# An attention and mixture-of-experts kernel: 48 expert tiles of five blocks first, results of three blocks read back early, ten half blocks at the end

## The chip, the cores and the metric

The kernel runs on one core of a Trainium2 chip, in one program. The metric is the device time of one execution in microseconds; lower is better. In the profile PE is TensorE (matmuls and transposes), PEld its weight loads, DVE is VectorE, ACT is ScalarE, POOL is GpSimd and SP is SyncE, which issues most DMAs. All arithmetic is in float32.

## The reference

The input x has 4 sequences of 1024 tokens with 256 features; the context has 4 sequences of 77 rows. Cut to what matters:

```python
h = layernorm(x)
x = x + cross_attention(h, ctx)        # 16 heads of 64, softmax over 77 keys, + h, a second layernorm
f = layernorm(x)                       # 4096 tokens
weights, indices = top_k(softmax(f @ Wg), 4)     # 32 experts
for e in range(32):
    pos = pairs (token, expert) with expert e, in order of token, at most 2048 of them
    xg = f[token of pos]
    y[token of pos] += (silu(xg @ W1[e]) * (xg @ W3[e]) @ W2[e]) * weight
z = silu(f @ Ws1) * (f @ Ws3) @ Ws2    # a shared expert, for every token
out = x + y + z
```

So there are 4096 × 4 = 16384 pairs of token and expert, and which pair goes to which expert is known only when the gate has been computed.

## The kernel before

**Blocks.** The 4096 tokens are 8 blocks of 512 (`NB`, `TB`), each of 4 chunks of 128. The first part of the program (lines 773 to 883, 32 steps `t`, one for each chunk) does the attention, and two blocks behind it the gate, the choice of four experts (`choose`, `mark`), the counting (`count`) and the placing (`place`) of every pair. `cums[b]` holds, for each expert, how many pairs the blocks before b have given it.

**Rows.** `send` (L685) scatters each token's normalised row to DRAM (`xr`), four times, once for each of its experts: 16 indirect DMAs for a block, issued by GpSimd. In `xr` each expert has its own stretch, filled in order of token.

**Expert tiles.** A tile is 128 rows of one expert. The expert part (lines 1222 to 1294) is a pipeline of four steps over tiles j: `expert_in` (two transposes on PE, gT copied by VectorE, L1131 and L1133), `expert_mid` (four matmuls L1139, silu on ScalarE, product h on VectorE), `expert_turn` (a transpose), `expert_out` (two matmuls L1163, the result scaled to y, and scattered by GpSimd to `ys` in DRAM, L1172, one row for each pair). In step j of the loop tile j is in `expert_in`, j − 1 in `expert_mid`, and so on. Rows come in groups of 8 tiles: `fetch` (L1077, on SP's queue, 8 DMAs, asked for 7 steps ahead), and `find` computes in three steps where each row's result goes (`place_`, L1118 or L1124).

**Two tables.** Which expert a tile belongs to and where its rows begin is computed on the chip, because it depends on the counts. Table "a" covers the first `NA` tiles. They are full tiles of rows of the first `BA` blocks, so that they may be fetched when the scatters of these blocks (`early`) have landed. Table "z" covers all later tiles, whose fetches wait for every scatter. An expert's last tile in it may be partly filled: it is read shifted back, and rows that came before are sent to places behind the results (`behind`, `again`, L1122 to L1124). Before the change `NA` is 64 and `BA` 6.

**Early results.** The tables put tiles with rows of the first `BE` blocks first: when `NE_` = `NA` + 32 tiles are done, all results of these blocks are in `ys`. Then they are read back: `take(i)` (L1194, on SP's queue, 512 KB: a chunk's 128 tokens with four results each) and `add_taken` (on VectorE: step 0 adds two pairs of results, L1204; steps 1 and 2 add the two sums to the residual `y0`, L1206). Three chunks are in flight; take i + 3 is issued behind the last add of chunk i. Before the change `BE` is 4, `NE_` 96, the takes begin in step 99, the adds in step 102, in turns of two and one a step. Up to tile `NE_` VectorE scales the results (L1168), from there on ScalarE (L1171).

**Number of tiles.** 128 tiles always run. How many more are needed depends on the counts; a Switch (L1276) goes to the code for that number. In this run it is 16 more, 144 in all.

**The end.** Behind the Switch (lines 1323 to 1360) the results of the blocks not taken early are read by half blocks: `gather` (L1307, 1 MB, on SP's queue, waits for all results) and `gathered` (three operations on VectorE, L1315 to L1317). Between them the shared expert of blocks 3, 4 and 5 is computed: `shared_in` (L715, PE), `shared_mid` (L730, VectorE), `shared_out` (L741, PE), `shared_add` (L754, VectorE). `store` writes half a block out, mostly on ScalarE's queue. Half block hb is half of block hb // 2.

**Order.** `as_written` makes every engine keep the order in which the program is written, except that neighbouring row scatters, and neighbouring result scatters, are free among themselves; operations of the end that need nothing from behind the Switch may be put ahead of it. In the program before, the last nine adds stand so on VectorE, beside tile 127.

Of the kernel before, what the change touches and what calls it, by code (L numbers as in the profile page):

```python
# [9 lines left out]
F32 = mybir.dt.float32  # L10
# [3 lines left out]
ALU = mybir.AluOpType  # L14
AX = mybir.AxisListType

P = 128
# [3 lines left out]
TOPK = 4  # L21
# [9 lines left out]
def kernel(  # L31
# [23 lines left out]
    nc = tc.nc  # L55
    T, D = x.shape
# [6 lines left out]
    NB = T // TB  # L63
# [4 lines left out]
    NJ = T * TOPK // P + NE  # L68


    NA, BA = 64, 6
    NM_ = T * TOPK // P


    BE = 4
    NE_ = NA + NE
    assert BE * TB * TOPK // P + NE <= NE_
    NV = 2 * NE
# [46 lines left out]
    for i in range(2):  # L125
# [13 lines left out]
    nc.gpsimd.memset(none, 0.0)  # L139
    nc.gpsimd.memset(none[:, IDX : IDX + TOPK], -1.0)  # L140
    nc.gpsimd.memset(none[:, OFF : OFF + 1], 1.0)
    behind = const.tile([P, NJ], F32, name="behind")
    nc.gpsimd.iota(
        behind,
        [[P, NJ]],
        base=T * TOPK,
        channel_multiplier=1,
        allow_small_or_imprecise_dtypes=True,
    )
# [623 lines left out]
    with as_written():  # L773
        for t in range(NT):
            blk, c = t // NC, t % NC
            ffn, old = blk - 1, blk - 2
            ahead = blk + 1 < NB
            if c == 0 and blk + 2 < NB:
                xts[blk + 2] = load(blk + 2)
            if t == 0:  # L780

                nc.sync.dma_start(xr[NE * PLACES :, :], none)
                nc.sync.dma_start(
                    xr[: NE * PLACES, :].rearrange("(e q) r -> q e r", q=PLACES)[:P],
                    none.unsqueeze(1).to_broadcast([P, NE, ROW]),
                )
            if t == 18:
                nc.sync.dma_start(ws13[:, :, 0, :], Ws1.rearrange("(k p) f -> p k f", p=P))
                nc.sync.dma_start(ws13[:, :, 1, :], Ws3.rearrange("(k p) f -> p k f", p=P))
                nc.sync.dma_start(ws2, Ws2.rearrange("(k p) f -> p k f", p=P))  # L790
            if t in parts:
                load_experts(*parts[t])
            if c == 1 and ahead:
                scale_in(blk + 1)
            if c == 1 and ffn >= 0:
                measure_out(ffn, 2, 4)
            if c == 3 and ahead:
                bias_in(blk + 1)
            if c == 3:
                measure_out(blk, 0, 2)  # L800
            if c == 3 and ffn >= 0:
                measure_ffn(ffn)
            if c == 1 and old >= 0:
                gate(old)
            if c == 3 and old >= 0:
                count(old)
            sv = [scores(t, g) for g in range(2)]
            if c == 1 and old >= 0:
                turn_gate(old)
                chances(old)  # L810
            soften(t, 0, sv[0])
            if c == 1 and old >= 0:
                powers(old)
            soften(t, 1, sv[1])
            sv.append(scores(t, 2))
            if t >= 1:
                for i in range(3):
                    turn_p(t - 1, i)
            soften(t, 2, sv[2])
            if c == 0 and old >= 0:  # L820
                turn_ffn(old)
            if c == 2 and ahead:
                turn_in(blk + 1)
            if c == 0 and ahead:
                measure_in(blk + 1)
            if c == 1 and old >= 0:
                choose(old)
            if c == 2 and old >= 0:
                mark(old)
            if c == 2 and old + 1 == BE:  # L830
                pairs_of("e", BE)
            if c == 3 and old >= 0:
                place(old)
            invert(t)
            divide(t)
            if c == 1 and ahead:
                norm_in(blk + 1)
            if c == 3 and ffn >= 0:
                norm_ffn(ffn)
            if c == 3:  # L840
                settle(blk, 0)
            elif ffn >= 0:
                settle(ffn, c + 1)
            if c >= 2 and ahead:
                keep(blk + 1, 2 * c - 4, 2 * c - 2)
            if t >= 11:
                b11, c11 = divmod(t - 11, NC)
                send(b11, c11 * TOPK, (c11 + 1) * TOPK)
            if t >= 1:
                residual(t - 1, output(t - 1))  # L850

        sxs[0] = late.tile([P, NC, D], F32, tag="qb", name="sx_0", bufs=3)
        sxs[0] = sxs[0].rearrange("p c d -> p (c d)").rearrange("p (k t) -> p k t", k=KC)
        nc.sync.dma_start(sxs[0], xnd[0])
        z, y = NB - 1, NB - 2
        assert BA == y
        pairs_of("a", BA)
        left = [(y - 1, i) for i in range(NK)]  # L860

        def sends(n):
            for blk, i in left[:n]:
                send(blk, i, i + 1)
            del left[:n]

        del left[:4]
        measure_out(z, 2, 3)
        settle(z, 1)
        sends(3)  # L870
        turn_ffn(y)
        for i in range(3):
            turn_p(NT - 1, i)
        settle(z, 2)
        residual(NT - 1, output(NT - 1))
        measure_out(z, 3, 4)
        gate(y)
        turn_gate(y)
        chances(y)
        powers(y)  # L880
        settle(z, 3)
        sends(2)
        measure_ffn(z)
# [202 lines left out]
    def find(j, step):  # L1086
# [17 lines left out]
        elif step == 1:  # L1104
            cw = bp.tile([P, RG, 2, TOPK], F32, tag="cw", name=f"cw_{j}")
            nc.vector.tensor_tensor(
                cw,
                g[:, :, CODE : CODE + 2 * TOPK].rearrange("p g (i k) -> p g i k", k=TOPK),
                n[1].unsqueeze(2).to_broadcast([P, RG, 2, TOPK]),
                ALU.mult,  # L1110
            )
            own = bp.tile([P, RG, 2], F32, tag="own", name=f"own_{j}")
            nc.vector.tensor_reduce(own, cw, AX.X, ALU.add)
            n.append(own)
        else:
            place_ = bp.tile([P, RG], I32, tag="place", name=f"place_{j}")
            if n[2] is None:
                nc.vector.tensor_copy(place_, n[3][:, :, 0])  # L1118
            else:

                far = bp.tile([P, RG], F32, tag="far", name=f"far_{j}")
                nc.vector.tensor_tensor(far, behind[:, j : j + RG], n[3][:, :, 0], ALU.subtract)  # L1122
                nc.vector.tensor_tensor(far, far, n[2], ALU.mult)
                nc.vector.tensor_tensor(place_, n[3][:, :, 0], far, ALU.add)  # L1124
            n.append(place_)
# [96 lines left out]
    with as_written():  # L1222
        fetch(0)
        fetch_shared(1, nc.sync)
        for j in range(NM_ + len(steps)):
# [23 lines left out]
                shared_out(1)  # L1249
            if j == 7:  # L1250
                shared_add(1)
            if NE_ + 6 <= j < NM_:
                for i, step in adds[: 1 + (j + 1) % 2]:
                    add_taken(i, step)

                    if step == TOPK // 2 and i % HC == 0 and HC <= i <= 2 * NC:
                        store(i // HC - 1, nc.sync)
                del adds[: 1 + (j + 1) % 2]
            if j < NM_ and j % RG in (0, 1, 2):
                find(j // RG * RG, j % RG)  # L1260
            if j == NM_ - 2 * RG:
# [10 lines left out]
                tc.switch_hint(more, (NJ - NM_) // RG + 1, label="more")  # L1272
            if j == NM_ + 2:
                fetch_shared(5, nc.scalar)
    ahead = groups[NM_ // RG][0]
    for n in tc.Switch(more, (NJ - NM_) // RG + 1, hint="more"):  # L1276
        end = NM_ + n * RG
# [20 lines left out]


    hs = ctx.enter_context(tc.tile_pool(name="hs2", bufs=2))  # L1300
    tl = ctx.enter_context(tc.tile_pool(name="tl", bufs=8))
    ysk = ys[: T * TOPK, :].rearrange("(b c p k) d -> b p c k d", c=HC, p=P, k=TOPK)

    def gather(hb):
# [13 lines left out]

    NS = NB - 2
    order = [*range(2 * NS, 2 * NB), *range(2 * BE, 2 * NS)]
    with as_written():
        come = [gather(hb) for hb in order]
        shared_in(3, 0, AF.Silu)
        shared_in(3, 1, AF.Silu)
        for i, step in adds:
            add_taken(i, step)
        shared_mid(3, 0)
        store(4)  # L1330
        shared_mid(3, 1)
        shared_in(4, 0, AF.Silu)
        store(5)
        shared_out(3)
        gathered(*come[0])
        shared_mid(4, 0)
        shared_in(4, 1, AF.Silu)
        shared_add(3)
        gathered(*come[1])
        shared_mid(4, 1)  # L1340
        for hb in (6, 7, 12, 13):
            store(hb)
        shared_in(5, 0, AF.Silu)
        shared_out(4)
        gathered(*come[2])
        shared_mid(5, 0)
        shared_in(5, 1, AF.Silu)
        gathered(*come[3])
        shared_add(4)
        shared_mid(5, 1)  # L1350
        for hb in (14, 15):
            store(hb)
        shared_out(5)
        gathered(*come[4])
        store(8)
        gathered(*come[5])
        store(9)
        gathered(*come[6])
        gathered(*come[7])
        shared_add(5, store)  # L1360


# [53 lines left out]
```

## Time and profile before

| what | value |
| --- | --- |
| time, median of 3 runs | 762.22 us (761.46 to 765.76) |
| the profiled execution's own time | 762.67 us |
| its span, first to last instruction | 760.9 us |
| mean granted TensorE clock | 0.990 |
| PE busy | 719.1 us, 95% |
| VectorE busy | 510.6 us, 67% |
| ScalarE busy | 356.7 us, 47% |
| GpSimd busy | 406.6 us, 53% |
| DMA | 111.98 MB, mean 147 GB/s |
| tiles 0 to 127 and the Switch | about 443 to 690 us of the span |
| the end behind the last tile | 717 to 760.9 us |

A row of a timeline reads: start in us from the span's start, length in us, engine, line, operation, what is written and read, how many; in brackets how long the engine was idle before it and what ended the idle time. A row of the DMA queue's waits reads: who waited, for whom, us in total, how often, the longest. Matmul ends are modelled, so PE counts as busy when it merely follows one matmul on another.

### The profile page before, as it was taken

The numbers are of one execution on the slowest core, as the hardware profiler recorded it, in microseconds if no ns is written. First come the engines' busy times: TensorE is split into PE (matmuls) and PEld (weight loads), VectorE is DVE, ScalarE is ACT, GpSimd is POOL, SyncE is SP. The second block draws the span as 40 slices with busy tenths as digits, with TensorE's granted clock in tenths as the row PEclk, the third lists the DMA queues.
The fourth block names the chain that finished last, engine by engine and source line by source line (L and its number), as shares of the span: only waits on it lengthen the run. The fifth ranks groups of instructions, "written<-read, shape, count | busy, mean of one in ns | idle before, by whom it ended". The sixth has DMA issues, their size and how long they took to land.

```text
span 760.9 us, 12980 instructions
## 1 busy us (share of the span) xinstructions
PE 719.1 (95%) x3512; PEld 535.7 (70%) x3512; DVE 510.6 (67%) x1447; ACT 356.7 (47%) x1634; POOL 406.6 (53%) x491
## 2 busy tenths in 40 slices
PE   6999999999999999999998999999999999988993
PEld 4775767677777777777674567888888887756762
DVE  1874476677787778786767646666677767754376
ACT  0647756676757766667652111222222234534410
POOL 2002344335877777777788775555565565533400
PEclk9999999999999999999999999999999999999997
DMA  8940000130416241331418644466655569962295
GB/s 281 331 127 1 0 1 2 29 110 31 149 44 224 82 135 55 96 109 59 156 53 254 208 150 137 135 193 207 201 164 167 170 221 312 312 227 74 75 398 206
DMA packets 78996, 111.98 MB, mean 147 GB/s; under 512 B 10124, under 2 KB 63808, under 8 KB 78912
## 3 DMA queue, kind: packets, MB, share of 16 engines
q1 hardware_dynamic: 61023, 68.24, 29.1%
q0 software_dynamic: 13056, 36.72, 13.2%
q10 hardware_dynamic: 4832, 6.07, 2.3%
q8 instruction: 32, 0.52, 0.3%
q14 instruction: 53, 0.43, 0.2%
HBM read 62.36 MB, written 48.64 MB: 146 GB/s over the span
## 4 chain that ended last, share of the span: by engine, by line
PE 72%; DVE 10%; ACT 6%; DMA 4%; POOL 3%; issue 3%; SPq 0%; DVEq 0%; POOLq 0%; ACTq 0%
PE po L508 15%; PE peh L1139 14%; PE sc L441 13%; PE py L1163 7%; PE ph L715 6%; ACT p L457 5%; PE pgT L1131 3%; PE pz L741 3%; PE phT L1153 2%; PE pp L490 2%; DVE mx L449 1%; DMA gx<-ys 1%; POOL xr L685 1%; PE pvo L273 1%; PE pvo L298 1%
## 5 line engine op out<-in xcount | busy, mean ns | idle before, releaser
L1172 POOL DMA_INDIRECT ys<-y,place x144 | 141.3, 982 | 118.0 <-ACT y L1171 46.4
L457 ACT ACTIVATE p<-sc,mx 128x77 f32<-128x77 f32 x512 | 159.5, 353 | 93.0 <-DVE mx L449 93.0
L1139 PE MATMUL peh<-we,gT 128*128 x576 | 150.4, 384 | 7.0 <-DVE gT L1133 7.0
L508 PE MATMUL po<-we,pT 128*128 128x256 f32 (+1 forms) x640 | 147.3, 383 | 4.6 <-DVE pT L495 4.3
L685 POOL DMA_INDIRECT xr<-xn,row x128 | 128.1, 1001 | 35.6 <-issue 32.7
L472 POOL TENSOR_TENSOR p<-p,su 128x385 f32<-128x385 f32 (+1 forms) x96 | 91.2, 976 | 97.2 <-DVE su L467 76.5
L441 PE MATMUL sc<-we,qT 128*128 128x385 f32 (+1 forms) x384 | 138.9, 509 | 0.9 <-POOL qT L427 0.9
L508 PEld LDWEIGHTS po<-we,pT 128*128 128x128 f32 (+1 forms) x640 | 118.4, 190 | 26.9 <-DVE pT L495 7.9
L1147 ACT ACTIVATE h<-peh 128x128 f32<-128x128 f32 x144 | 39.9, 278 | 173.1 <-PE peh L1139 165.4
L457 ACT ACTIVATION_READ_ACCUMULATOR p<-sc,mx 128x1 f32 x512 | 119.6, 234 | 0.0
L1139 PEld LDWEIGHTS peh<-we,gT 128*128 128x128 f32 x576 | 98.8, 191 | 17.5 <-DVE gT L1133 9.2
L441 PEld LDWEIGHTS sc<-we,qT 128*128 128x128 f32 x384 | 71.1, 189 | 54.3 <-issue 27.7
L1148 DVE TENSOR_TENSOR h<-peh,h 128x128 f32<-128x128 f32 x144 | 41.8, 290 | 70.8 <-ACT h L1147 70.3
L1163 PE MATMUL py<-we,ehT 128*128 x288 | 86.5, 383 | 0.0
L449 DVE TENSOR_REDUCE mx<-sc 128x5 f32<-128x385 f32 (+1 forms) x96 | 54.4, 576 | 33.3 <-PE sc L441 32.4
L1133 DVE COPY gT<-pgT 128x256 f32<-128x256 f32 x144 | 59.8, 416 | 12.6 <-PE pgT L1131 12.6
L1131 PE MATMUL pgT<-ident,g 128*128 128x128 f32 x288 | 55.2, 274 | 0.8 <-PE py L1163 0.5
L1163 PEld LDWEIGHTS py<-we,ehT 128*128 128x128 f32 x288 | 43.8, 192 | 11.9 <-issue 1.0
L1131 PEld LDWEIGHTS pgT<-ident,g 128*128 128x128 f32 x288 | 40.2, 141 | 16.6 <-issue 2.2
L1168 DVE TENSOR_SCALAR y<-py,own 128x256 f32<-128x256 f32 x96 | 46.4, 483 | 0.1
L490 PEld LDWEIGHTS pp<-ident,p 128*128 128x128 f32 x320 | 36.1, 139 | 11.4 <-issue 5.5
L715 PE MATMUL ph<-sx,ws 128*128 128x512 f32 x96 | 42.9, 595 | 0.0
(221 smaller groups left out, 945.2 us busy)
## 6 DMA issues: line engine op xcount, KB each, us to landing
g<-xr SPq DMA_DIRECT2D x144, 136.0 KB
gx<-ys SPq DMA_DIRECT2D x16, 512.0 KB
gy<-ys SPq DMA_DIRECT2D x8, 1024.0 KB
xr<-y SPq DMA_DIRECT2D x1, 4352.0 KB
y<-in_x SPq DMA_DIRECT2D x8, 512.0 KB
xnd<-xnT SPq DMA_DIRECT2D x6, 512.0 KB
we<-in_W SPq DMA_DIRECT2D x8, 384.0 KB
out<-y ACTq DMA_DIRECT2D x12, 256.0 KB
```

The source lines that it names most:

```text
L441: nc.tensor.matmul(sc[:, : (h1 - h0) * SK], qTs[blk][:, k, o : o + P], mq[:, b, k, h0 * SK : h1 * SK], start=(k == 0), stop=(k == KC - 1),)
L449: nc.vector.tensor_reduce(mx[:, h0:h1], sv, AX.X, ALU.max, negate=True)
L457: nc.scalar.activation(probs[t][:, h, :], sv[:, h - h0, :], AF.Exp, bias=mx[:, h : h + 1], accum_out=su[:, h : h + 1],)
L472: nc.gpsimd.tensor_tensor(p[:, h0:h1, :], p[:, h0:h1, :], su[:, h0:h1].unsqueeze(2).to_broadcast([P, h1 - h0, SK]), ALU.mult,)
L508: nc.tensor.matmul(po[:, :D], pT[:n, i, :], vo[b][:n, i, :], start=(i == 0), stop=(i == KT - 1))
L685: sct = nc.gpsimd.indirect_dma_start(out=xr, out_offset=bass.IndirectOffsetOnAxis(ap=row[:, i : i + 1], axis=0), in_=xn[:, c, :], in_offse ...
L715: nc.tensor.matmul(ph[i], ws13[:, k, i, f * P : (f + 1) * P], xnT[:, k, :], start=(k == 0), stop=(k == KC - 1),)
L1131: nc.tensor.transpose(pt[:, k * P : (k + 1) * P], g[:, j % RG, k * P : (k + 1) * P], ident)
L1133: nc.vector.tensor_copy(gT.rearrange("p k t -> p (k t)"), pt[:, :D])
L1139: nc.tensor.matmul(ph[:, : 2 * H], gT[:, k, :], we[:, ds(ev[j] * EW + k * 2 * H, 2 * H)], start=(k == 0), stop=(k == KC - 1),)
L1163: nc.tensor.matmul(py[:, :D], hT, we[:, ds(ev[j] * EW + KC * 2 * H, D)], start=True, stop=True)
L1172: sent = nc.gpsimd.indirect_dma_start(out=ys, out_offset=bass.IndirectOffsetOnAxis(ap=place_[:, i : i + 1], axis=0), in_=y, in_offset=None,)
```

## The change

`NA` goes from 64 to 48, `BA` from 6 to 5 and `BE` from 4 to 3, so `NE_` from 96 to 80. The counts for table "a" are copied when the placing of block 4 is marked (in step t = 26), no longer after the attention loop. `behind` is held only for the tiles of table "z", and is read by the position in that table. The takes begin in step 83, the adds in step 88, one a step; 36 adds, the last in step 123. None are left for the end. The half blocks 6 and 7 (block 3) are now gathered at the end, ten in all, in the order 12, 13, 6, 7, 14, 15, 8, 9, 10, 11, with ten buffers. Stores follow their half blocks.

```diff
-    NA, BA = 64, 6
+    NA, BA = 48, 5
     NM_ = T * TOPK // P
-    BE = 4
+    BE = 3
...
-    behind = const.tile([P, NJ], F32, name="behind")
+    behind = const.tile([P, NJ - NA], F32, name="behind")
     nc.gpsimd.iota(
         behind,
-        [[P, NJ]],
-        base=T * TOPK,
+        [[P, NJ - NA]],
+        base=T * TOPK + NA * P,
...
-            if c == 2 and old + 1 == BE:
-                pairs_of("e", BE)
+            if c == 2 and old + 1 in (BE, BA):
+                pairs_of("e" if old + 1 == BE else "a", old + 1)
...
-        assert BA == y
-        pairs_of("a", BA)
...
-                nc.vector.tensor_tensor(far, behind[:, j : j + RG], n[3][:, :, 0], ALU.subtract)
+                nc.vector.tensor_tensor(far, behind[:, jt : jt + RG], n[3][:, :, 0], ALU.subtract)
...
-            if NE_ + 6 <= j < NM_:
-                for i, step in adds[: 1 + (j + 1) % 2]:
+            if NE_ + 8 <= j < NM_:
+                for i, step in adds[:1]:
                     add_taken(i, step)
...
-                del adds[: 1 + (j + 1) % 2]
+                del adds[:1]
...
-    tl = ctx.enter_context(tc.tile_pool(name="tl", bufs=8))
+    tl = ctx.enter_context(tc.tile_pool(name="tl", bufs=10))
...
-    order = [*range(2 * NS, 2 * NB), *range(2 * BE, 2 * NS)]
     with as_written():
-        come = [gather(hb) for hb in order]
+        come = {hb: gather(hb) for hb in (12, 13, 6, 7, 14, 15, 8, 9, 10, 11)}
         shared_in(3, 0, AF.Silu)
         shared_in(3, 1, AF.Silu)
-        for i, step in adds:
-            add_taken(i, step)
         shared_mid(3, 0)
         store(4)
         shared_mid(3, 1)
         shared_in(4, 0, AF.Silu)
         store(5)
         shared_out(3)
-        gathered(*come[0])
+        gathered(*come[12])
         shared_mid(4, 0)
         shared_in(4, 1, AF.Silu)
         shared_add(3)
-        gathered(*come[1])
+        gathered(*come[13])
         shared_mid(4, 1)
-        for hb in (6, 7, 12, 13):
-            store(hb)
+        store(12)
+        store(13)
         shared_in(5, 0, AF.Silu)
         shared_out(4)
-        gathered(*come[2])
+        gathered(*come[6])
         shared_mid(5, 0)
         shared_in(5, 1, AF.Silu)
-        gathered(*come[3])
+        gathered(*come[7])
         shared_add(4)
         shared_mid(5, 1)
-        for hb in (14, 15):
+        store(6)
+        store(7)
+        shared_out(5)
+        for hb in (14, 15, 8, 9):
+            gathered(*come[hb])
             store(hb)
-        shared_out(5)
-        gathered(*come[4])
-        store(8)
-        gathered(*come[5])
-        store(9)
-        gathered(*come[6])
-        gathered(*come[7])
+        gathered(*come[10])
+        gathered(*come[11])
         shared_add(5, store)
```

More of the change, by code (lines that the diff above doesn't have):

```diff
@@ L1274 @@
                 fetch_shared(5, nc.scalar)
+    assert not adds
     ahead = groups[NM_ // RG][0]
@@ L1317, in gathered @@
         nc.vector.tensor_tensor(y, y, g[:, :, 1, :], ALU.add)
-    NS = NB - 2
-    order = [*range(2 * NS, 2 * NB), *range(2 * BE, 2 * NS)]
     with as_written():
-        come = [gather(hb) for hb in order]
+        come = {hb: gather(hb) for hb in (12, 13, 6, 7, 14, 15, 8, 9, 10, 11)}
         shared_in(3, 0, AF.Silu)
         shared_in(3, 1, AF.Silu)
-        for i, step in adds:
-            add_taken(i, step)
         shared_mid(3, 0)
```

## The prediction

> **What bounds the kernel now.** I read the page's slices first (PE is 90% busy or more in almost every one), then the busy time of each engine stage by stage, then PE's order of time where it is not full, then VectorE's order of time at the end.
>
> The stages, in the order of columns stretch, length, PE, PEld, DVE, ACT, POOL, clock, DMA share, GB/s:
>
> ```profile
> core 0: us, PE busy (x) PEld busy (x) DVE busy (x) ACT busy (x) POOL busy (x), PEclk, DMA share, GB/s
> ...
> 385.00:444.00 59.00, 52.68 (x235) 33.36 (x233) 38.78 (x134) 18.54 (x61) 47.51 (x60) 1.00 0.58 190
> ...
> 480.00:612.00 132.00, 132.00 (x732) 111.53 (x731) 92.17 (x296) 35.13 (x162) 77.71 (x81) 1.00 0.57 179
> 612.00:673.00 61.00, 56.19 (x300) 45.77 (x299) 44.52 (x140) 28.22 (x97) 35.56 (x34) 1.00 0.90 295
> 673.00:690.00 17.00, 13.22 (x44) 7.43 (x43) 7.47 (x22) 3.78 (x11) 3.12 (x3) 0.95 0.54 156
> ...
> 717.00:749.00 32.00, 31.52 (x98) 18.07 (x96) 20.03 (x26) 4.16 (x8) 1.92 (x2) 1.00 0.88 337
> 749.00:761.00 12.00, 0.00 (x0) 0.00 (x0) 7.93 (x11) 0.00 (x0) 0.00 (x0) 0.67 0.26 91
> ```
>
> From 480 to 612 PE is never idle: the expert tiles run at PE's pace. From 612 to 673, where results of the first four blocks are read back and added, PE loses 4.8 us and the DMA share is 0.90. In the last 12 us PE is done and VectorE works alone. So two places can move: the stretch of the taken results, and the end.
>
> PE's order of time gives the price of the first place:
>
> ```profile
> 616.22 1.03 PE L1139 MATMUL peh<-we,gT 128*128 x4
> ...
> 626.66 1.13 PE L1139 MATMUL peh<-we,gT 128*128 x4 [0.51 <-DVE gT L1133]
> ...
> 649.31 1.13 PE L1139 MATMUL peh<-we,gT 128*128 x4 [0.75 <-DVE gT L1133]
> ...
> 668.09 1.03 PE L1139 MATMUL peh<-we,gT 128*128 x4
> 671.59 1.13 PE L1139 MATMUL peh<-we,gT 128*128 x4 [1.93 <-DVE gT L1133]
> ```
>
> These are tiles 97, 103, 115, 126 and 127. Undisturbed a tile takes 1.6275 us (tile 13 at 479.51 to tile 97 at 616.22: 84 steps). From 616.22 to 668.09 there are 29 steps, 47.20 us at that pace; they took 51.87. The last step took 3.50, where 1.41 would do (no further tile is turned in, 0.22 less). Together 4.67 + 2.09 = 6.76 us lost. Tiles 112 and 113 (642.76 and 645.03; 0.67 and 0.64 too late) come behind the loading of `more` and the hint for the Switch, at the end of step 112; these 1.31 us stay. The other 5.4 us hang on the takes: VectorE waits for the first one (0.67), has two adds in every other step (0.69 and 0.42 us beside 0.42 for gT and 0.29 for h, some ten steps at 0.03 to 0.44), waits in L1124 (0.92, 0.53) and, at the last step, for takes 13 to 15 (2.09; their nine adds stand ahead of h of tile 127 on VectorE).
>
> The end, on VectorE:
>
> ```profile
> 744.91 0.69 DVE L730 TENSOR_TENSOR hT<-ph,sg 128x512 f32<-128x512 f32 x1 [2.42 <-PE ph L715]
> 745.51 1.22 DVE L1315 TENSOR_TENSOR gy<-gy 128x1024 f32<-128x1024 f32 x1
> 746.76 0.69 DVE L1316 TENSOR_TENSOR y<-y,gy 128x512 f32<-128x512 f32 x1
> 747.49 0.69 DVE L1317 TENSOR_TENSOR y<-y,gy 128x512 f32<-128x512 f32 x1
> 748.10 1.22 DVE L1315 TENSOR_TENSOR gy<-gy 128x1024 f32<-128x1024 f32 x1
> ...
> 755.86 1.28 DVE L754 TENSOR_TENSOR y<-pz,y 128x512 f32<-128x512 f32 x2
> ```
>
> PE hands over the last half of block 5 at 744.9. Behind it stand four half blocks, 2.59 us each (745.51 to 748.10), then the shared expert's sum, and 3.8 us for the last store. This is a bare chain: whatever is added behind 744.91 is paid in full.
>
> **The change, part by part.** The profiled execution took 762.67 us for a span of 760.9; the median of the runs is 762.22, 0.45 less. I sum against the profiled execution and carry the difference over.
>
> *Fewer blocks ahead of the first tile: 0.* The first fetch no longer needs the twelve row scatters of block 5, but they were not what it waited for:
>
> ```profile
> SPq L1055 <- DVE r_tab_a L981: 17.7, 1, 17.7
> ```
>
> SP waited for the table of offsets and issued at 426.44; the tiles then wait for PE, which comes to them in its own order at 443.54. The PE order is the same in both programs up to the tables' widths. All scatters are issued by 459.3 on POOL, and the first fetch that now needs all of them (tile 48) is issued in step 41, at about 523: no new wait. The number of tiles stays 144, since tiles that no longer come first come later.
>
> *Tables 16 columns narrower and wider.* The nine operations on the later table (0.25 to 0.39 us, 468.86 to 471.27) stand ahead of gT, for which PE is 1.47 us idle. Between 0 and a sixth of their 2.4 us: I take +0.2.
>
> *Tiles 48 to 63 are placed by the longer form.* Three more operations (0.16 to 0.17 us) in each of two groups, 1 us of VectorE, which is 70% busy there while PE is full: 0.
>
> *Tiles 80 to 95 are scaled on ScalarE.* 16 × 0.47 us; with 0.28 and 0.26 it does 1.0 us of a 1.63 us step, as tiles 96 to 127 show already: 0.
>
> *Takes from step 83, one add a step from 88.* At step 99 the first take was issued at 621.03, behind tile 95's result, and landed 4.0 us later; the first add, in step 102, was ready at 624.4 and waited. Sixteen steps (26.0 us) sooner it is issued at about 595.0 and lands at 599; the first add now stands five steps behind, not three, at 601.6. That wait goes, with 2.6 us to spare. Later takes are asked for seven steps ahead (11 us; before, under five). VectorE has 0.71 us of gT and h and one add of 0.69 or 0.42 in a step of 1.63, so the double adds go, and the nine late ones with their 2.09 us too. DMA: 12 takes are 6.3 MB in 36 steps, 107 GB/s, a share of 0.26 at the 410 GB/s of the end; four stores add 0.04 to the 0.57 of the stage before: 0.87, spread over 59 us. What stays: L1124 waits for the results in flight once ScalarE makes y (the two waits above, for a result that took 3.34 us to land; with 2.4 us, the median, it would not have waited), now in five groups and not three. Behind it on VectorE stands the next tile's gT, and PE waits for that. With one add in the step I put 0.2 to 0.3 on each, 1.3 us in all. Gain 5.4 − 1.3 = 4.1; bounds 5.4 (nothing left) and 2 (all five cost what the two long ones did).
>
> On SP a take waits for the buffer that the add frees, and fetches queue behind it; a group of g is asked for seven steps ahead of its first tile, so 0 as long as a fetch is not held up by more than some 7 us (11 us less the 4 that its eight issues take).
>
> *Ten half blocks at the end.* Half blocks 12, 13, 6 and 7 take the places that four others had ahead of 744.9, so exactly two more, 2 × 2.59 = 5.2 us, stand behind it. Their DMA: 10 gathers and six stores, 12.1 MB, at the 410 GB/s that the end shows from 724 on:
>
> ```profile
> 736.00:738.00 2.00, 2.00 (x7) 0.98 (x6) 1.79 (x3) 0.60 (x1) 0.00 (x0) 1.00 1.04 417
> ```
>
> From 723 that is 29 to 31 us: all landed by 754, with the last one due at 745.5 + 5 × 2.59 = 758.5. Hidden by 4 us. SP's waits before the later gathers (4.7 and 5.0 us, for the second gather and the second store) move to gathers eight to ten and leave six in flight. [...]
>
> Sum: −4.1 + 0.2 + 5.2 = +1.3. Profiled 764.0, median 763.5 us.
>
> **The rivals.**
>
> *Slower: the takes find the DMA full anyway (0.17).* Place: steps 83 to 124. For it: 295 GB/s already meant a share of 0.90, a result then took 3.34 us to land, and fetches come eight at a time. It decides once the share passes 0.95 there; then waits at L1124 and for gx return and the gain falls to between 0 and 1.5. Price +3.9 to +5.4: 766.1 to 767.6. Against it: 0.57 with 179 GB/s is far from full.
>
> *Slower: the end becomes DMA's (0.08).* The two more gathers share the engines with stores on ScalarE's queue; if the last lands after 758.5, each us late is a us more. Two to four late: 765.5 to 767.5. Against: the 4 us of slack.
>
> *Faster: the stop after the Switch shrinks (0.12).* ScalarE is idle for 5.33 us from 681.6, PE 3.16 of it, and the matmul after it took 2.05 us, not 1.03, under a clock of 0.92. Without it 3.4 + 1 us go: about 759. ScalarE has sixteen more instructions ahead of the Switch now, and SP comes to it earlier, without takes before it. [...]
>
> *The change does not start tiles sooner (as I forecast) but a start shows after all (0.03).* It could take the 1.7 us that PE idles at 468 to 472: 761.8.
>
> **How the numbers follow.** Forecast 0.60, at 763.5, its own range 762 to 766 (gain 2 to 5.4). The range reaches to the rivals on both sides: 759.5 to 767.4. Half a per cent, 3.8 us, is what a measurement can tell here: under 758.4 or over 766.0. Faster 0.07: half of the Switch's case and a little. Slower 0.18: three quarters of the two slower rivals' 0.25. Same 0.75.
>
> **What would show it.** Right: tiles 97 to 127 take about 50 to 51 us, not 55.4; no wait of DVE for gx; PE's first tile at 443.5 ± 0.5; six half blocks behind the last L730, VectorE's end to the span's end again 3.8 us. Wrong: a wait for gy before the last half blocks; a DMA share over 0.95 from 595 to 660; a first expert tile sooner by more than 1 us; a stop after the Switch that differs by more than 1 us from 3.2.

## The result, and the profile after

Run side by side, the kernel before took 765.72 us and the changed one 760.42 us, medians of ten runs each: ratio 0.9935, 95% interval 0.9911 to 0.9959. It is faster by 0.65%, where 763.5 (no change) was forecast. The profiled execution of the changed kernel took 760.35 us, its span is 758.6.

Four windows of the changed kernel, to set beside those of before:

```profile
core 0: us, PE busy (x) PEld busy (x) DVE busy (x) ACT busy (x) POOL busy (x), PEclk, DMA share, GB/s
385.00:444.00 59.00, 54.05 (x222) 33.09 (x221) 38.19 (x132) 18.84 (x61) 47.40 (x61) 0.91 0.58 188
...
612.00:660.00 48.00, 47.36 (x260) 39.34 (x259) 32.84 (x110) 26.02 (x87) 27.57 (x29) 1.00 0.86 274
673.00:690.00 17.00, 16.18 (x73) 11.31 (x72) 7.18 (x23) 6.74 (x20) 4.78 (x5) 1.00 0.31 100
717.00:749.00 32.00, 24.37 (x81) 14.78 (x79) 26.28 (x34) 2.39 (x4) 0.00 (x0) 0.93 0.98 387
```

Three things stand here. Between 612 and 660 PE is now full (47.36 of 48; before, 56.19 of 61 from 612 to 673). In the 17 us around the Switch, PE is busy 16.18, not 13.22. And in the first row the granted clock is 0.91, where it was 1.00: PE came to the tiles 3.5 us later. That last point belongs to the execution and not to the change: in a later profile of the same front (tenth run, below; mean granted clock 0.993, here 0.980) PE turned in its first tile at 443.86, in the kernel before at 443.54. So stretches are compared from the first tile on.

| stretch, us | before | after | difference | forecast |
|---|---|---|---|---|
| first product of tile 0 (at) | 444.81 | 448.28 | +3.5 (clock) | +0.0 |
| to that of tile 127 | 226.78 | 221.38 | −5.4 | −4.1 + 0.2 |
| to the end's first L715 | 45.52 | 40.30 | −5.2 | 0 |
| to VectorE's last instruction | 40.03 | 45.21 | +5.2 | +5.2 |
| to the end of the span | 3.74 | 3.39 | −0.4 | 0 |

From the first tile on: −5.8 us, where 1.3 us more were forecast; the medians differ by 5.3. Two stages gained over five microseconds each, and the longer end gave one of them back.

PE's timeline, tiles 97, 113, 126 and 127 (start, duration, engine, line):

```profile
619.84 1.03 PE L1137 MATMUL peh<-we,gT 128*128 x4
...
645.46 1.03 PE L1137 MATMUL peh<-we,gT 128*128 x4
...
668.25 1.03 PE L1137 MATMUL peh<-we,gT 128*128 x4
669.66 1.03 PE L1137 MATMUL peh<-we,gT 128*128 x4
```

Tile 97 to 127 took 49.8 us, not 55.4, and the last step 1.41, not 3.50. VectorE no longer waits for a taken block at all. It is the stretch behind that was not foreseen. ScalarE's timeline at the Switch, first in the kernel before, then in the changed one; the last row of each is the first expert tile behind the Switch:

```profile
681.14 0.47 ACT L1171 ACTIVATE y<-py,own 128x256 f32<-128x256 f32 x1 [1.55 <-PE py L1163]
...
686.94 0.45 ACT L1147 ACTIVATE h<-peh 128x128 f32<-128x128 f32 x2 [5.33 <-SPq L1412]
```

```profile
679.11 0.47 ACT L1169 ACTIVATE y<-py,own 128x256 f32<-128x256 f32 x1 [1.55 <-PE py L1161]
...
681.41 0.28 ACT L1145 ACTIVATE h<-peh 128x128 f32<-128x128 f32 x1 [1.83 <-PE peh L1137]
```

Before, ScalarE sat idle for 5.33 us and then had two tiles waiting for it (x2). After, it waits 1.83 us, and for PE's product, as any tile does. The trace's branch records say the same: from ScalarE's branch to the first instruction at its target 5.0 us before, 0.5 after. The bracket's releaser, SP, is the last signal seen, not the cause: SP reached its own branch at 672.7 us before, nine microseconds earlier.

PE waited 3.16 us for this in the kernel before, and behind that wait the granted clock was 0.50 for 3.4 us, in which a tile's four products took 2.05 us, not 1.03:

```profile
688.30:691.70 3.40, 3.29 (x9) 2.57 (x10) 1.19 (x6) 0.68 (x3) 0.00 (x0) 0.50 0.01 2
```

By estimate, from that 0.50, half of these 3.4 us, 1.7, are lost. The wait and this spell make up 4.9 of the 5.2 us by which the stretch shrank; the changed kernel's profile has neither.

The end, on VectorE:

```profile
737.76 0.69 DVE L730 TENSOR_TENSOR hT<-ph,sg 128x512 f32<-128x512 f32 x1 [2.41 <-PE ph L715]
738.37 1.21 DVE L1314 TENSOR_TENSOR gy<-gy 128x1024 f32<-128x1024 f32 x1
...
753.89 1.28 DVE L754 TENSOR_TENSOR y<-pz,y 128x512 f32<-128x512 f32 x2
```

The second row begins the first of six half blocks, and the last row follows the sixth. None of the six waits, and 2.41 us of idle time stand in front of the first row.

### The profile page after: what moved, and what is told of

Same layout as the page of the kernel before. It is cut to its first block, busy times and chain, and to the rows that moved or that the text cites. A ratio compares the mean times of both kernels' runs of the same rounds, so it can differ in the third digit from the quotient of the medians.

```text
span 758.6 us, 12990 instructions
## 1 busy us (share of the span) xinstructions
PE 719.1 (95%) x3512; PEld 536.8 (71%) x3512; DVE 504.5 (67%) x1431; ACT 364.3 (48%) x1650; POOL 402.4 (53%) x491
## 4 chain that ended last, share of the span: by engine, by line
PE 78%; DVE 9%; ACT 6%; POOL 2%; DMA 2%; issue 1%; SPq 0%; DVEq 0%; ACTq 0%
PE peh L1137 16%; PE po L508 15%; PE sc L441 13%; PE py L1161 8%; PE ph L715 7%; ACT p L457 5%; PE pgT L1129 4%; PE pz L741 3%; PE phT L1151 2%; PE pp L490 2%; PE pvo L273 2%; DVE mx L449 1%; POOL xr L685 1%; PE pvo L298 1%; PE pm L273 1%
## 5 line engine op out<-in xcount | busy, mean ns | idle before, releaser
L1170 POOL DMA_INDIRECT ys<-y,place x144 | 137.6, 956 | 113.8 <-ACT y L1169 43.6
L1137 PE MATMUL peh<-we,gT 128*128 x576 | 148.8, 381 | 3.3 <-DVE gT L1131 3.2
L715 PE MATMUL ph<-sx,ws 128*128 128x512 f32 x96 | 45.7, 626 | 0.0
L490 PE MATMUL pp<-ident,p 128*128 128x128 f32 x320 | 40.7, 273 | 0.9 <-POOL p L472 0.9
```

The source lines that it names most:

```text
L490: nc.tensor.transpose(pp[:n, (c - c0) * P : (c - c0 + 1) * P], p[:, c * P : c * P + n], ident)
L715: nc.tensor.matmul(ph[i], ws13[:, k, i, f * P : (f + 1) * P], xnT[:, k, :], start=(k == 0), stop=(k == KC - 1),)
L1137: nc.tensor.matmul(ph[:, : 2 * H], gT[:, k, :], we[:, ds(ev[j] * EW + k * 2 * H, 2 * H)], start=(k == 0), stop=(k == KC - 1),)
L1170: sent = nc.gpsimd.indirect_dma_start(out=ys, out_offset=bass.IndirectOffsetOnAxis(ap=place_[:, i : i + 1], axis=0), in_=y, in_offset=None,)
```

## The experiments

The question is why ScalarE's stop behind the Switch went. **Theory 1**: it hangs on the place of ScalarE's code in its program, which the sixteen scalings (with as many waits) moved. **Theory 2**: it came, in the kernel before, from the transfers that crowded that stretch (DMA share 0.54 from 673 to 690 us, 0.31 in the changed kernel). The expectations speak of code that is loaded or fetched; that is the author's supposition, and no trace shows what ScalarE waits for. Positions are instructions counted in ScalarE's program, waits and register instructions included; every trace has 516 records more up to the branch, so the differences are the same there.

All but runs 9 to 11 were on chips where the kernel before took 793 to 795 us, at mean granted clocks of 0.963 to 0.976 (runs 9 to 11: 764.25 us, 0.979 to 0.993), so stretches are compared. Tiles 0 to 127 are slower there as well: 223.3 to 223.4 us with the changed kernel's loop (runs 8, 14 and 15), 228.2 to 228.9 with that of before (runs 2, 5, 7 and 13) and once 230.5 (run 12), a gain of about 5 us. In runs 4 and 6 the granted clock was still 0.50 for 10 us among the first tiles, and they took 233.5 and 236.3. On the chip of runs 9 to 11 the changed loop took 221.9 and 221.7 and the one before 225.7 (run 11), a gain of about 4.

**1. Scalings back on VectorE**

```
-        if j < NE_:
+        if j < NE_ + 16:
             nc.vector.tensor_scalar(y, py[:, :D], own[:, i, 1:2], None, ALU.mult)
```

> The changed kernel, but the results of tiles 80 to 95 are scaled on VectorE again, as in the kernel before; all else stays. Theory 1 (whether an engine finds the code behind the Switch loaded depends on where that code lies in its program, and the sixteen scalings, with as many waits, moved ScalarE's code): ScalarE's stop after the Switch comes back, about 5 us from its branch to the first instruction behind it instead of 0.5, PE idles about 3 us there again and the time from tile 127 to the first product of the end grows from 40.3 towards 45.5 us, so the whole is 3 to 5 us slower than the changed kernel, about 762 to 765. Theory 2 (the code was fetched late because transfers crowded the stretch around the Switch in the kernel before): the stop stays away (40.3 us, ScalarE's branch 0.5 us), time as the changed kernel's within 1 us. In both, the scaling itself costs nothing: tile 0 to tile 127 stays 221.4 us within 1 us.

```profile
708.68 0.47 ACT L1169 ACTIVATE y<-py,own 128x256 f32<-128x256 f32 x1 [1.55 <-PE py L1161]
...
713.80 0.45 ACT L1145 ACTIVATE h<-peh 128x128 f32<-128x128 f32 x2 [4.64 <-SPq L1406]
```

The stop is back: 4.64 us idle and two tiles queued, 4.3 us from the branch to its target, the stretch 44.8 us. The transfers are the changed kernel's, so theory 2 has no reason for it. The whole took 793.39 us, ratio to the kernel before 0.9972 (0.9934 to 1.0009): with the stop, the gain is gone. Tiles 0 to 127 took 223.6, so the scalings themselves cost no more than 0.3 us on either engine.

**2. Scalings on ScalarE in the kernel before**

```
-        if j < NE_:
+        if j < NE_ - 16:
             nc.vector.tensor_scalar(y, py[:, :D], own[:, i, 1:2], None, ALU.mult)
```

> The kernel before, but the results of tiles 80 to 95 are scaled on ScalarE, as in the changed kernel: one part of the change alone. Theory 1 (place of the code): ScalarE's stop after the Switch goes, 5.0 to about 0.5 us, the time from tile 127 to the first product of the end falls from 45.5 to about 40.3 to 42 us, and the whole is 3 to 5 us faster than the kernel before. Theory 2 (crowded transfers): the transfers are those of before, so the stop stays (45.5 us) and the time is the kernel before's within 1 us.

The stop went (0.5 us from branch to target), the stretch took 41.3 us, and the ratio is 0.9928 (0.9892 to 0.9964): this one line alone brings about what the whole change brings. What stays over 40.3 us is a wait of PE for the first fetched rows behind the Switch (1.0 us); this kernel still has its late takes.

**3. One and two adds a step in turn**

```
-                for i, step in adds[:1]:
+                for i, step in adds[: 1 + (j + 1) % 2]:
...
-                del adds[:1]
+                del adds[: 1 + (j + 1) % 2]
```

> The changed kernel, but one and two adds a step in turn from tile 88, as the kernel before did from its own start, instead of one. If the pace is what took the waits away (prediction's step e), the stalls of PE at the place conversions come back for the 24 steps in which the 36 adds then run: tile 0 to tile 127 grows from 221.4 by 2 to 4 us, to 223.5 to 225.5, and VectorE waits for results of tiles still underway. If the waits of before came from its place among tiles 102 to 127 alone (the loading of the count, the hint and the third-from-last fetches), nothing grows: 221.4 within 0.7 us. ScalarE's code keeps the place that it has in the changed kernel within three instructions, so by theory 1 the stop behind the Switch stays away.

Tiles 0 to 127 took 226.8 us, 3.5 over the 223.3 of the chip. PE's timeline, tiles 98 to 100:

```profile
647.73 1.13 PE L1137 MATMUL peh<-we,gT 128*128 x4
...
651.47 1.44 PE L1137 MATMUL peh<-we,gT 128*128 x4 [1.05 <-DVE gT L1131]
...
654.19 1.71 PE L1137 MATMUL peh<-we,gT 128*128 x4
```

One tile waited for VectorE's gT, and the products behind it ran slow (1.44 and 1.71, not 1.03 us) while the granted clock was 0.50:

```profile
652.20:655.60 3.40, 3.40 (x11) 2.57 (x10) 1.73 (x5) 1.01 (x3) 1.43 (x2) 0.50 0.97 359
```

By estimate, from that 0.50, half of these 3.4 us, 1.7, are the clock's; that the wait brought the clock down is not shown. The stop behind the Switch stayed away, at 0.5 us. So in this profile the pace of one add a step holds 1.8 to 3.5 of the 5 us by which the tiles became faster; the rest is left to the earlier start and the shorter list, which were not tried apart. 788.56 us, ratio 0.9927 (0.9891 to 0.9962): the ratio is that of the changed kernel, so the runs as a whole do not show what the pace is worth.

**4. Half block 14 into VectorE's wait**

```
         shared_add(4)
+        gathered(*come[14])
         shared_mid(5, 1)
...
-        for hb in (14, 15, 8, 9):
+        store(14)
+        for hb in (15, 8, 9):
```

> The changed kernel, but the fifth half block of the end (14) is added ahead of the last product of gate and value instead of behind it, into the 2.41 us in which VectorE waits for PE there. If VectorE's chain sets the end, as the prediction's step f has it, the last VectorE instruction comes 2.4 us sooner less the 0.2 us by which that product is late: about 2.2 us, span 756.4 against 758.6. If DMA sets the end (gathers and stores at the rate that they have), the gather of this half block or of the last one is waited for and the gain is under 1 us.

```profile
758.48 0.69 DVE L1316 TENSOR_TENSOR y<-y,gy 128x512 f32<-128x512 f32 x1
759.09 0.68 DVE L730 TENSOR_TENSOR hT<-ph,sg 128x512 f32<-128x512 f32 x1
759.69 1.21 DVE L1314 TENSOR_TENSOR gy<-gy 128x1024 f32<-128x1024 f32 x1
...
772.63 1.28 DVE L754 TENSOR_TENSOR y<-pz,y 128x512 f32<-128x512 f32 x2
```

The idle time in front of L730 is gone and five half blocks stand behind it. From the end's first product to VectorE's end: 42.7 us, not 45.2. VectorE's chain sets the end, as the prediction had it. 783.83 us, ratio 0.9885 (0.9833 to 0.9937).

**5 to 7. ScalarE's code shifted, and nothing else.** Copies of one element a partition ahead of all of ScalarE's work, in the kernel before; only their number differs:

```
+    spare = const.tile([P, 32], F32, name="spare")
+    for i in range(31):
+        nc.scalar.copy(spare[:, i % 32 : i % 32 + 1], ones[:, i % 32 : i % 32 + 1])
     measure_in(0)
```

> The kernel before with 31 copies of one element a partition added on ScalarE ahead of all its work; the tiles, their transfers and the engines that scale them are the kernel before's. They put ScalarE's code for the Switch 31 instructions further on, which is where the kernel with its scalings on ScalarE (second experiment) has it. Theory 1 (place of the code): ScalarE's stop of 5.0 us behind the Switch goes to about 0.5, and tile 127 to the first product of the end takes 40.3 to 41.5 us, not 45.5. Rival (the scalings mattered through the times of the late tiles, not through the place): late tiles are the kernel before's, so the stop stays at 4.3 to 5.0 us and the stretch at 45 us.

> The same with 200 such copies. [...] With the branch at 1649 and the target at 1704 no edge lies between: no stop, 0.5 us. [...]

> [...] Place theory with that period: the stop of 4.3 to 5.0 us is back. Rival (more instructions ahead help whatever their number): no stop, 0.5 us.

ScalarE with 31 copies:

```profile
713.29 0.47 ACT L1174 ACTIVATE y<-py,own 128x256 f32<-128x256 f32 x1 [1.55 <-PE py L1166]
...
716.08 0.28 ACT L1150 ACTIVATE h<-peh 128x128 f32<-128x128 f32 x1 [2.31 <-PE peh L1142]
```

No stop, though scalings, tiles and transfers are the kernel before's: the place decides, theory 1, and the rival with the times of the late tiles falls. The stretch took 40.9 us. With 200 and 240 copies there was no stop either (0.5 us each). The stretch took 42.9 and 42.3 us: in both the granted clock was 0.50 for 3.4 us ahead of the Switch, and with 200 copies ScalarE waited 2.1 us some tiles behind it. An edge, in these expectations, is a place in ScalarE's code, again every 256 instructions, that brings the stop when it lies between branch and target. All of this was supposed, the 256 too; no run had shown it. With the stop at branches 1450 and 1452 and none at 1481 and 1484, one edge would lie at 1453 to 1481 and the next at 1709 to 1737, between branch (1689) and target (1744) of the run of 240. That run has no stop, which contradicts it.

**8. Two half blocks on GpSimd**

```
+        gathered(*come[15], nc.gpsimd)
+        gathered(*come[8], nc.gpsimd)
         store(14)
-        for hb in (15, 8, 9):
+        gathered(*come[9])
...
```

(Lines are set against the fourth run.)

> The changed kernel with half block 14 ahead of the last product as in the fourth experiment, and half blocks 15 and 8 added on GpSimd, which has nothing to do in the end, instead of VectorE. GpSimd's products of 128x385 took 974 ns, so an estimate for 128x1024 and two of 128x512 is 2.6 and twice 1.3 us, 5.2 a half block and 10.4 for both, from about 734 to 745 us in the changed kernel's times. If VectorE's chain sets the end, three half blocks are left behind the last product and its end comes 2.2 + 2 x 2.59 = 7.4 us sooner less what it waits for the last gathers (DMA busy until 747: at least 3 us of it), so 3 to 5 us sooner than the changed kernel. If the two engines get in each other's way, VectorE's 1.22 and 0.69 us grow and the gain is the 2.4 us of the fourth experiment or less.

The L1315 additions by engine (minimum, median and maximum in ns):

```profile
L1315 DVE TENSOR_TENSOR y<-y,gy x8: 691/692/2718, 749.1 to 781.0; 128x512 f32<-128x512 f32 x8
L1315 POOL TENSOR_TENSOR y<-y,gy x2: 1592/1594/1597, 767.4 to 774.0; 128x512 f32<-128x512 f32 x2
```

While GpSimd added (764.7 to 777.3 us), VectorE's additions of 0.69 us took 1.63 to 2.72 and those of 1.22 took 1.68 and 2.28, and behind that 0.69 and 1.22 again: the two got in each other's way, and the end took 45.0 us. The gain of the fourth run went, too. 788.49 us, ratio 0.9932 (0.9894 to 0.9970). Over what the two meet, the trace does not show.

**9. The changed kernel again**

> The changed kernel itself, unedited, on this chip, where the clock falls lower ahead of the tiles than on the chip of the first comparison: the reference for the experiments. By the place theory its stretches are those that it had: tile 0 to tile 127 221.4 us where the clock is full (the experiment with the scalings back on VectorE had 223.6, so this says what of that is the scalings' and what the chip's), tile 127 to the first product of the end 40.3, from there to VectorE's end 45.2. If the stop's absence was luck of one profile, the second stretch is 45 us here.

On a chip like the first, not the one meant: 759.56 us, ratio 0.9932 (0.9906 to 0.9959). Stretches 221.9, 40.4 and 45.2 us, ScalarE's branch 0.5 us: the first profile was no luck. One thing differs. TensorE's own branch took 3.5 us in this execution and 0.4 in the first, of the same program; the stretch is 0.1 us longer.

**10. Two half blocks summed on TensorE**

```
+                for k in range(TOPK if summed else 0):
+                    nc.tensor.matmul(pz[:, c * D : (c + 1) * D], ident, summed[c2][:, c, k, :],
+                                     start=False, stop=(k == TOPK - 1))
...
-        gathered(*come[10])
-        gathered(*come[11])
```

> The changed kernel with half block 14 ahead of the last product, as in the fourth experiment, and half blocks 10 and 11 summed on TensorE: sixteen products of the gathered rows with the identity, onto the last block's outputs that lie in PSUM, so VectorE adds them with the two additions that it does anyway. Behind the last L730 VectorE has three half blocks (7.8 us) and the two additions (1.3 us) left, not six; the products take 16 x 0.23 = 3.6 us from when the gathers land (about 747 us in the changed kernel's times). If VectorE set the end, this is 2.2 + 2 x 2.59 = 7.4 us sooner; since the last gather bounds it at about 747 + 2 + 1.3, 751 against 755.2, I expect 4 to 5 us: span to end of VectorE from the end's first product 40 to 41 us, not 45.2.

Half block 14 stands as in the fourth run. PE's first products, then VectorE's two additions:

```profile
741.40 3.78 PE L749 MATMUL pz<-gy,ident 128*128 128x256 f32 x8 [4.95 <-DMA gy<-ys]
```

```profile
748.64 0.69 DVE L762 TENSOR_TENSOR y<-pz,y 128x512 f32<-128x512 f32 x1 [5.17 <-PE pz L749]
753.82 0.69 DVE L762 TENSOR_TENSOR y<-pz,y 128x512 f32<-128x512 f32 x1 [4.49 <-PE pz L749]
```

A miss: 47.4 us, and 761.26 us in all, ratio 0.9959 (0.9939 to 0.9978). Each of the 16 products is two records of 0.24 us (the second eight took 1.92), so it costs twice the 0.23 that I reckoned, and the last two half blocks are the ones that land last: PE sat 4.95 us waiting for them and then stood in VectorE's way, which idled 5.2 and 4.5 us for it. The granted clock was also 0.50 from 739.9 to 746.7 us; the first eight records, in it, took 3.78 us and the next eight 1.92. The mean granted clock was 0.993, and the front is not late: the first tile came at 443.86 us, the tiles took 221.7, the Switch's stretch 40.3.

**11 to 13. Further shifts**

> The kernel before with 496 copies ahead of ScalarE's work (branch at instruction 1944, target at 1999). The edge with a period of 256 fell with the run of 240. With a period of 512, which the runs so far leave standing (stop at branches 1450 and 1452; none at 1481, 1484, 1649 and 1689), an edge lies at 1965 to 1993 and the stop of 4.3 to 5.0 us is back. If there is no such period, ScalarE goes on after 0.5 us, and the rule behind the place stays open.

> The kernel before with 257 copies ahead of ScalarE's work, which puts its branch at instruction 1706: 256 on from where the kernel before has it. If the stop hangs on the place within pieces of 256 instructions (the runs so far allow it: by the remainder, stops at 170 and 172, none at 113, 152, 153, 201, 204), the stop of 4.3 to 5.0 us is back and tile 127 to the first product of the end takes 44 to 46 us. If not, ScalarE goes on after 0.5 us and that stretch takes 40.5 to 43.

> The same with 516 copies: branch at instruction 1964, by the remainder of 256 at 172, where the experiment with the scalings back on VectorE had the stop. Period of 256: the stop is back, 4.3 to 5.0 us. No stop here but one in the run with the branch at 1706, or the reverse: something besides the remainder counts. None in both: no such period, and the rule stays open.

With 496 copies there was no stop (0.5 us). ScalarE with 257 copies (branch at 1706), then with 516 (1964):

```profile
719.92 0.47 ACT L1174 ACTIVATE y<-py,own 128x256 f32<-128x256 f32 x1 [1.55 <-PE py L1166]
...
724.93 0.45 ACT L1150 ACTIVATE h<-peh 128x128 f32<-128x128 f32 x2 [4.54 <-SPq L1415]
```

```profile
736.54 0.47 ACT L1174 ACTIVATE y<-py,own 128x256 f32<-128x256 f32 x1 [1.55 <-PE py L1166]
...
741.36 0.45 ACT L1150 ACTIVATE h<-peh 128x128 f32<-128x128 f32 x2 [4.35 <-SPq L1415]
```

Both have the stop, 4.2 and 4.0 us by the branch records. The stretch took 44.6 us in both; PE waited 2.0 and 1.7 us for ScalarE in it, and a spell of 3.4 us at a granted clock of 0.50, ahead of the stop, holds another 1.5 to 1.7 by estimate. All positions of ScalarE's branch, by the remainder of 256:

| remainder | position (kernel) | branch to target |
|---|---|---|
| 113 | 1649 (200 copies) | 0.5 us |
| 152, 153 | 1944 (496), 1689 (240) | 0.5 |
| 170 | 1450 (before), 1706 (257) | 5.0, 4.2 |
| 172 | 1452 (scalings back), 1964 (516) | 4.3, 4.0 |
| 201 | 1481 (scalings in before; 31; two a step) | 0.5 |
| 204 | 1484 (changed; runs 4, 8 to 10, 14 and 15) | 0.5 |

256 instructions further on (1450 to 1706) and 512 (1452 to 1964) the stop is there again, so a period of 256 fits; 128 or 64 would fit these positions as well, and no run tells them apart. With 256, the stretch of positions that stops is narrower than the 48 between 153 and 201. One count goes with the stop: in the 9 us behind ScalarE's branch the page's instruction queue (q14) carried seven packets of 8192 bytes in each of the four profiles with the stop and six in each of the thirteen without. Which engine a packet is for is not marked, so that ScalarE waits for code is not shown. What it waits for, and why only at these positions, is open.

**14 and 15. The end, shorter**

> The kernel of the fourth experiment again, on the chip of this call, to set beside the next run: from the end's first product to VectorE's end 42.7 us as before, against 45.2 in the changed kernel; as the changed kernel is 0.9932 of the kernel before, 2.5 us less than that is 0.990.

> The same, and half block 15 summed on TensorE into a bank of its own (products of the gathered rows with the identity, 32 records, 3.8 us as the tenth run had them, in which TensorE has nothing else to do), with one addition of 0.69 us left to VectorE in place of 2.59. If VectorE's chain sets the end, 42.7 - 1.9 = 40.8 us from the end's first product to VectorE's end; the last gather, which landed about 37 us after that product in the tenth run (start of the products that waited for it), leaves 37 + 2.6 + 1.3 = 41 as the bound, so 40.8 to 41.5, and 0.988 of the kernel before. If the products start late or run long, no gain over the run before.

The first repeats the fourth run: 42.7 us, 783.71, ratio 0.9897 (0.9832 to 0.9961). The second, with half block 15 in a bank of its own:

```
+        pg = products(*come[15])
         store(14)
-        for hb in (15, 8, 9):
+        for hb in (8, 9):
             gathered(*come[hb])
             store(hb)
+        summed(15, pg)
+        store(15)
```

(Lines are set against the first.)

```profile
774.45 0.69 DVE L1315 TENSOR_TENSOR y<-pg,y 128x512 f32<-128x512 f32 x1 [1.27 <-PE pg L1307]
```

42.5 us, not 40.8: I put its addition ahead of half block 10 on VectorE, where it waited 1.27 us for PE, most of the 1.9 that it saved. 780.51 us, ratio 0.9853 (0.9791 to 0.9916). These are the lowest ratios of the study, but their intervals overlap that of the changed kernel; only the 2.5 to 2.7 us of the end are shown.

## Why the prediction was wrong, step by step

- **Fewer blocks ahead of the first tile: 0.** Right where the clock did not fall: 443.86 in the tenth run (mean granted clock 0.993) against 443.54 (0.990). In the changed kernel's own profile the clock of 0.91 put it at 447.0, outside the 443.5 ± 0.5 that I gave; the prediction took the 1.00 of its own windows as given.
- **Tables, place form, scalings on ScalarE: +0.2, 0, 0.** Nothing in the tiles speaks against the three as costs. But the last one was the step that failed, below.
- **Takes and adds: −4.1.** The mechanism was right. The size was −5.4, my upper bound, in the first profile, and −4.9 with the ninth run in its place; against run 11, on the ninth run's own chip, it is −3.8, so 4.1 lies within what the runs show. The 1.3 us that I left for L1124 (now L1122) do not show: VectorE waited there for results in flight twice in the whole program, 0.2 us each, and PE's steps at the first of them were 0.2 us too long in all. The DMA share was 0.85 from 595 to 660, as forecast (0.87), so the rival with the full DMA did not come.
- **Ten half blocks: +5.2.** Right to the digit: 40.03 to 45.21, six half blocks behind the last L730 without a wait for gy, and the transfers hidden. The rival with the DMA's end did not come. Only the last store was 0.4 us shorter.
- **The stop behind the Switch: 0 in the sum, 0.12 as a rival.** This is the step that failed: −5.2 us for the stretch, of which 3.2 are PE's wait for ScalarE and 1.7, by estimate, the spell at a clock of 0.50 behind it. The prediction saw the stop, and that ScalarE had sixteen more instructions ahead of it, and still summed with a stop that stays; that was the author's estimate, and no run shows it. The runs show that the stop hangs on the position: shifting ScalarE's code alone takes the stop away (5.0 us to 0.5) and brings 45.5 us to 40.9, and shifting it by 256 brings the stop back. Such a spell is not the stop's alone: runs 6 and 7 had one of 3.4 us at 0.50 in this stretch without the stop. Of the 0.6 to 1.0 us that runs 5 and 2 then have over 40.3, the second run shows PE waiting 1.0 us for fetched rows behind the Switch, with the late takes still there; this part was not tried by itself. "SP comes to it earlier" was not the reason: SP's branch came at 672.7 before and at 660.4 after, and with the scalings back on VectorE it is as early and the stop is there.

The forecast +1.3 against a measured −5.8 from the first tile on: 5.2 of it are the Switch's stretch, 1.5 the takes with the tables, 0.4 the last store.

## What to carry to other kernels

An edit can pay or cost at a place that it does not touch, as here by moving an engine's code (5.0 us or 0.5 from ScalarE's branch to its target): where a branch shows a stop of some microseconds, count that engine's instructions, ask what the edit does to the count, and give a change of the stop its own chance, not a small one. To see whether it is that, put harmless instructions ahead of the engine's work and vary their number. And a gain off the last stage's chain can be given back there: the end here grew by exactly the half blocks that the chain took on, while 2.4 us of idle time in front of them stayed unused.

## What the runs showed of the hardware that was not expected

- ScalarE's branch into the Switch's code, to a target 55 instructions on, took 0.5 us in thirteen profiles and 4.0 to 5.0 in four, by its position: 4.0 to 5.0 at instructions 1450, 1452, 1706 and 1964, 0.5 at 1481, 1484, 1649, 1689 and 1944. From branch to target SP took 3.1 to 3.8 us and GpSimd 4.2 to 5.1 in every profile, VectorE 0.6; TensorE took 0.4 to 4.4, in one program both 0.4 and 3.5. In the kernel before its 3.3 us (677.7 to 680.9) passed while PE ran products (L715, 677.1 to 680.7). A hint of the branch stood 34 to 41 us ahead of it on ScalarE, and the stops came all the same.
- While GpSimd added, VectorE's additions of 0.69 us took as much as 2.72 (eighth run).
- The granted clock was 0.50 for 3.4 us at a time among the late tiles or behind the Switch in seven profiles (before and runs 1, 3, 6, 7, 12 and 13), each time during a wait of PE or within 2 us behind one of 1.05 to 3.29 us. A wait of 1.93 us in the kernel before passed without it, so no rule is shown.
- The clock ahead of the tiles fell in one execution and not in another: between 385 and 444 us it was 0.91 in the changed kernel's first profile (0.50 for 10.2 us from 413.6) and 1.00 in the kernel before. In the tenth run, whose front is the changed kernel's, the mean over the span was 0.993, not 0.980, and the first tile came 3.1 us sooner (443.86, not 447.00).
